# TensorE's instruction order fixed to the order of tracing beside five MLP blocks of a two-layer transformer kernel

## The chip, the cores and the metric

The kernel runs on one core of one Trainium2 chip, as one program in one launch. The metric is the device time of that launch in microseconds, the median of several runs. The profiled execution is one more run; its own time stands beside its span below.

The engines are called by the profile's names: PE is TensorE (matmuls), PEld its weight loads, DVE is VectorE, ACT ScalarE, POOL GpSimd, SP the engine that issues all loads and stores here. Each works through a list of its own, in order; where one needs a result of another it waits on a semaphore.

## The reference

Two layers over 2,048 tokens (32 sequences of 64) of width 512, everything in float32. Cut to what matters:

```
# layer 0: rms norm scaled by a condition, 8 query heads of 64 on one key head, rope, then a gated MLP
h = ada_rms(x, cond, ln1_w, ln1_tw)
q, k, v = h @ Wq.T, h @ Wk.T, h @ Wv.T
x = x + softmax(rope(q) @ rope(k).T / 8) @ v @ Wo.T
h = ada_rms(x, cond, ln2_w, ln2_tw)
x = x + (silu(h @ Wg.T) * (h @ Wu.T)) @ Wd.T          # inner width 2048
# layer 1: layer norm with scale and shift from the condition, 16 heads of 32 on 4 latent key heads
h = (x - mean(x)) * rsqrt(var(x) + eps) * (1 + scale) + shift
c = h @ Wkd.T;  k, v = c @ Wku.T, c @ Wvu.T;  q = h @ Wq.T
out = x + softmax(masked(rope(q) @ rope(k).T / sqrt(32))) @ v @ Wo.T
```

Each sequence attends to itself alone, so scores and contexts are many small products.

## The kernel before, in words

**Tiling.** The tokens are cut into eight units of 256 (four sequences each), kept transposed: features on the partitions, tokens along the row. A unit goes through `attention0` (layer 0), then the MLP, then `attention1` (layer 1). The MLP works on blocks, `BLOCKS = ((0,), (1, 2), (3, 4), (5, 6), (7,))`: three blocks of two units and a block of one at either end.

**The MLP.** Each weight product is done by seven products of half size instead of eight (the names `P1` to `P7`), with sums of weight quarters and of inputs prepared by DVE and POOL. `gate_up_first` issues the four EARLIER products of a group and the partial sums that follow (line 1068 on ACT, lines 1069, 1070 and 1089 on DVE). `gate_up_last` issues the three LATER ones, which add onto the same PSUM regions and so have to wait until those sums have been read; then come line 1098 and 1107 on DVE, `silu` (1101, 1102) on ACT and `gated` (1109 to 1112) on POOL. `down` does the same for the third weight, with `gu` and `down` as names of the PSUM tiles. All of these matmuls are issued by line 1053, in `multiply`. In block 0 DVE also makes the sums of the weights (lines 331 to 334) and the rotation angles of later units (line 421).

**Narrow matmuls.** Scores (`sc`: line 792 in layer 0, 982 in layer 1) and contexts (`cx`: 813 and 1012) contract over 64 rows only. They are traced so that neighbours differ in the half of the rows they use: the score loops go over `for r, sc in enumerate(banks)` innermost, with `of = slice(r * HD0, (r + 1) * HD0)`, and so do the contexts. Between scores and contexts lies the softmax: lines 654, 655, 662, 663 on DVE, 660 on ACT, the scaling 664 on POOL (tile `p`), then the transposes `pp` on PE (669) and the copy `pT` on ACT (670). The output product is `po` (line 634), the context copies `cT` are 823 and 1024.

**What sets the order.** Three things. First the tracing: `Order.run` takes pieces from generators (`mlp(j)`, `attention0` of the units of the next block, and the `chain` of `attention1` of units that are finished), each with a cost and a latency written by hand, and so interleaves their instructions. Second the framework's scheduler: it makes from what was traced the list of each engine, and may put an instruction ahead of others that were traced before it when it takes those to be not ready yet. Third the helper `ordered(tc, engine)`: it ties every instruction of that engine, traced inside it, to the one traced before, with a dependence that needs no semaphore, so that the scheduler has to keep their order:

```
    for one, other in zip(mine, mine[1:]):
        tc.add_manual_dep(other, one.name, info, reason="order")
```

Before the change it is used on PE in two places, around the hand-written orders `FIRST` (the head) and `LAST` (the tail), and on SP for the first loads. The five calls of `order.run` beside the MLP blocks (line 1305) are not inside it: there the scheduler moves PE's instructions. The lists of the other engines are the scheduler's in either kernel, and so are SP's, whose weight loads wait for the matmuls that free their slots.

Of the kernel before, what the change touches and what calls it, by code (L numbers as in the profile page):

```python
# [103 lines left out]
@contextmanager  # L104
def ordered(tc, engine):

    traced = tc.nc.cur_bb.bb.instructions
    start = len(traced)
    yield
    mine = [i for i in traced[start:] if i.engine == engine]  # L110
    info = mybir.DependencyInfo(mybir.DependencyClass.NoSync, mybir.DependencyReason.DATA)
    for one, other in zip(mine, mine[1:]):
        tc.add_manual_dep(other, one.name, info, reason="order")
# [18 lines left out]
def two_blocks(ctx: ExitStack, tc: tile.TileContext, a: dict, out: bass.AP):  # L132
# [328 lines left out]
    def turning():  # L461
        for i, units in enumerate(TURNED):
            yield from angles(units, 4.0 if i else 1.5)
            if i + 1 < len(TURNED):
                load_positions(TURNED[i + 1])
# [702 lines left out]
    def mlp(j):  # L1168
        cost = 1.8 if len(BLOCKS[j]) == 1 else 3.5
        for g in GROUPS:  # L1170
            gate = gate_up_first(j, 0, g[0])
            yield cost, 0.0
            up = gate_up_first(j, 1, g[0])
            yield cost, 0.0
            for q in g:
                gate_up_last(j, 0, q, *gate)
                silu(gate[0], gate[2])
                yield 0.75 * cost, 0.0
                more = None
                if q != g[-1]:  # L1180
                    more = gate_up_first(j, 0, q + 1)
                    yield cost, 0.0
                gate_up_last(j, 1, q, *up)
                gated(j, q, up[0], up[2], gate[2])
                yield 0.75 * cost, 0.0
                gate = more
                if q != g[-1]:
                    up = gate_up_first(j, 1, q + 1)
                    yield cost, 0.0
            yield from down(j, g)  # L1190
# [3 lines left out]
    order = Order()  # L1194
# [47 lines left out]
    rest = [ahead, Job(turning(), 1.0)]  # L1242
# [31 lines left out]
    def some(pieces, n):  # L1274

        for cost, latency in pieces:
            n -= cost > 0
            yield cost, latency
            if not n:
                return  # L1280

    def in_turn(units):
        for u in units:
            while u not in x_units or u not in turned_units:
                yield 0.0, 1.0
            yield from attention0(u, {"ring": "0"})

    chain = Job(behind(), 0.8 * A1)
    for j, units in enumerate(BLOCKS):
        now = Job(mlp(j), M * len(units))  # L1290
        jobs = [now, *rest]
        must = [now]
        if j == 0:
            must.append(ahead)
        if j + 1 < len(BLOCKS):
            more = [u for u in BLOCKS[j + 1] if u > 1]
            must.append(Job(in_turn(more), A0 * len(more)))
            jobs.append(must[-1])
        if j == 1:
            jobs.append(chain)  # L1300
        if j == len(BLOCKS) - 1:
            jobs.append(Job(some(sixth, EARLY), 5.0))
        chain.total = 0.8 * A1 * (len(BLOCKS[j - 1]) if j else 1)
        chain.done = 0.0
        rest = order.run(jobs, until=tuple(must))
    order.run(rest)
    homes["now"] = everywhere
    room7 = {
# [100 lines left out]
```

## Time and profile before

| what | value |
|---|---|
| median of 3 runs | 1018.92 us (1017.89 to 1021.43) |
| the profiled run's own time | 1017.48 us |
| its span, from the first to the last instruction | 1015.7 us |
| PE busy | 985.1 us (97%), 6,710 records |
| DVE / POOL / ACT busy | 543.5 / 426.0 / 300.5 us |
| PE idle, all waits | some 30 us |
| mean granted clock of PE | 0.995 |

Stretches of 25 us show where PE is not full (the rest of the span between 200 and 825 us has it at 24.2 or more of 25):

| stretch, us | PE busy | DVE busy | granted clock |
|---|---|---|---|
| 0 to 50 (head) | 44.8 of 50 | 37.6 | 1.00 |
| 75 to 100 (block 0) | 21.1 of 25 | 23.4 | 1.00 |
| 125 to 150 (block 0) | 20.4 | 24.6 | 0.94 |
| 150 to 175 (block 0) | 22.0 | 18.0 | 0.92 |
| 825 to 850 (end of block 3) | 21.9 | 3.9 | 0.93 |
| 1000 to 1016 (tail) | 11.6 of 16 | 3.7 | 1.00 |

How to read it: times are from one execution. A float32 matmul leaves two records, a transpose one, so "x32" of scores are 16 matmuls. The ends of matmul records are modelled and overlap the next start; durations of stretches are therefore taken here from start to start. A 128x256 product takes 0.432 us from its start to the next one's (two records of 0.216), a 128x128 one 0.223 us.

### The profile page before, as it was taken

What the parts mean: (1) busy time and instruction counts of PE and PEld (TensorE: products, weight loads), DVE (VectorE), ACT (ScalarE), POOL (GpSimd) and SP (SyncE); (2) the same over time, 40 slices, a digit from 0 to 9 for tenths busy, and PEclk for the clock granted to TensorE, in tenths of its full rate; (3) what the DMA queues carried; (4) which work ended last, traced back from release to release, by engine and by line L of the source; (5) the groups of instructions that cost most, each with busy time, mean ns of one, the idle gap of its engine ahead of it and who ended that gap; (6) DMA issues with size and microseconds to landing.
All of it is one profiled execution on the core that took longest, in us unless ns stands there. A gap on an engine that the chain in (4) does not pass through costs nothing.

```text
span 1015.7 us, 17477 instructions
## 1 busy us (share of the span) xinstructions
PE 985.1 (97%) x6710; PEld 853.2 (84%) x6710; DVE 543.5 (54%) x1188; ACT 300.5 (30%) x550; POOL 426.0 (42%) x439
## 2 busy tenths in 40 slices
PE   8998988999999999999999999999999989999998
PEld 7788878988888888888888887888788869998986
DVE  5779997665364342654455361564335533654274
ACT  4434133123223211234313341322413321425032
POOL 5336265444523333534344333554234523843251
PEclk9999999999999999999999999999999999999999
DMA  7936375623222345222232234323233324746201
GB/s 272 325 126 218 128 230 173 211 88 132 72 69 83 130 138 171 86 94 85 94 115 94 73 124 129 120 89 120 80 95 107 130 88 158 248 157 222 90 2 42
DMA packets 82642, 132.23 MB, mean 130 GB/s; under 512 B 8832, under 2 KB 48512, under 8 KB 82176
## 3 DMA queue, kind: packets, MB, share of 16 engines
q1 hardware_dynamic: 82560, 131.12, 38.9%
q8 instruction: 53, 0.87, 0.3%
q14 instruction: 29, 0.24, 0.1%
HBM read 114.31 MB, written 16.78 MB: 129 GB/s over the span
## 4 chain that ended last, share of the span: by engine, by line
PE 83%; DVE 9%; DMA 2%; POOL 2%; issue 2%; ACT 2%; SPq 0%; POOLq 0%; DVEq 0%; ACTq 0%
PE gu L1053 34%; PE down L1053 17%; PE po L634 10%; PE q L634 10%; PE sc L982 2%; DVE stays L421 2%; PE pp L669 2%; PE lat L634 1%; DMA stays<-in_wmlp 1%; PE cx L1012 1%; PE kv L634 1%; ACT cT L823 1%; PE cx L813 1%; PE sc L792 1%; PE tab L502 1%
## 5 line engine op out<-in xcount | busy, mean ns | idle before, releaser
L1053 PE MATMUL gu<-h,stays 128*128 128x256 f32 (+1 forms) x1280 | 259.9, 341 | 10.5 <-issue 5.6
L1053 PEld LDWEIGHTS gu<-h,stays 128*128 128x128 f32 x1280 | 207.7, 191 | 36.3 <-issue 12.0
L1053 PE MATMUL down<-stays 128*128 128x256 f32 (+1 forms) x1120 | 210.2, 341 | 0.0
L1053 PEld LDWEIGHTS down<-stays 128*128 128x128 f32 x1120 | 177.2, 191 | 24.2 <-issue 5.4
L1053 PE MATMUL gu<-hc,stays 128*128 128x256 f32 (+1 forms) x960 | 195.5, 339 | 0.4 <-DVE hc L860 0.2
L1053 PEld LDWEIGHTS gu<-hc,stays 128*128 128x128 f32 x960 | 157.5, 191 | 17.4 <-DVE hc L860 0.6
L634 PE MATMUL po<-cT,stays 128*128 128x256 f32 x480 | 109.5, 385 | 2.8 <-ACT cT L823 2.6
L634 PE MATMUL q<-h,stays 128*128 128x256 f32 x480 | 109.2, 380 | 0.0
L634 PEld LDWEIGHTS po<-cT,stays 128*128 128x128 f32 x480 | 91.5, 193 | 16.9 <-ACT cT L823 3.9
L1109 POOL TENSOR_TENSOR stays<-gate,stays 128x768 f32<-128x768 f32 (+1 forms) x40 | 53.1, 1329 | 113.6 <-DVE stays L1098 106.8
L634 PEld LDWEIGHTS q<-h,stays 128*128 128x128 f32 x480 | 90.2, 190 | 11.9
L1068 ACT COPY e<-gu 128x256 f32<-128x256 f32 (+1 forms) x80 | 26.1, 328 | 188.7 <-PE gu L1053 188.6
L664 POOL TENSOR_TENSOR p<-p,sm 128x512 f32<-128x512 f32 x40 | 41.7, 1059 | 89.5 <-DVE sm L663 88.1
L645 POOL TENSOR_TENSOR qT<-u_q,v_q 128x512 f32<-128x512 f32 x30 | 38.1, 1271 | 87.6 <-DVE v_q L644 87.6
L690 DVE TENSOR_TENSOR x<-x,po 128x512 f32<-128x512 f32 x28 | 19.2, 687 | 102.3 <-PE po L634 102.3
L1069 DVE TENSOR_TENSOR u<-e,gu 128x256 f32<-128x256 f32 (+1 forms) x80 | 28.8, 360 | 62.6 <-ACT e L1068 62.6
L621 POOL TENSOR_TENSOR h<-x,stays 128x1024 f32<-128x1024 f32 x12 | 23.0, 1914 | 66.9 <-DVE x L690 48.8
L1110 POOL TENSOR_TENSOR stays<-stays 128x512 f32<-128x512 f32 (+1 forms) x40 | 45.0, 1126 | 4.1 <-DVE stays L1107 1.4
L1070 DVE TENSOR_TENSOR w<-u,gu 128x256 f32<-128x256 f32 (+1 forms) x80 | 29.1, 364 | 31.0 <-PE gu L1053 30.3
L576 DVE RECIPROCAL stays<-stays 128x256 f32<-128x256 f32 (+1 forms) x23 | 35.4, 1540 | 14.6 <-ACT stays L575 14.5
L654 DVE TENSOR_REDUCE mx<-sc 128x8 f32<-128x512 f32 (+1 forms) x52 | 31.4, 642 | 20.9 <-PE sc L982 16.9
L1098 DVE TENSOR_TENSOR gate<-gu,u 128x512 f32<-128x512 f32 (+1 forms) x40 | 23.2, 580 | 32.8 <-PE gu L1053 32.4
(223 smaller groups left out, 1268.6 us busy)
## 6 DMA issues: line engine op xcount, KB each, us to landing
stays<-sums SPq DMA_DIRECT2D x96, 384.0 KB, 3.0
stays<-in_wmlp SPq DMA_DIRECT2D x120, 256.0 KB, 3.0
stays<-in_wmlp SPq DMA_DIRECT2D x120, 128.0 KB, 2.5
stays<-sums SPq DMA_DIRECT2D x96, 128.0 KB, 2.3
sums<-stays SPq DMA_DIRECT2D x24, 384.0 KB, 3.0
mod<-in_mod SPq DMA_DIRECT2D x8, 512.0 KB, 5.2
x<-in_x SPq DMA_DIRECT2D x8, 512.0 KB, 5.8
a<-in_wmlp SPq DMA_DIRECT2D x24, 128.0 KB, 3.4
```

Of the source, the lines that this page charges most:

```text
L576: nc.vector.reciprocal(r, r)
L634: nc.tensor.matmul(ps, w[:, k, cols], h[:, k, :], start=(k == 0), stop=(k == KC - 1))
L645: nc.gpsimd.tensor_tensor(dst, u, v, ALU.add)
L654: nc.vector.tensor_reduce(mx, s3, AX.X, ALU.max)
L664: nc.gpsimd.tensor_tensor(p8, p8, sm.unsqueeze(2).to_broadcast(wide), ALU.mult)
L1053: nc.tensor.matmul(ps[REGION[p]][:, c], w[:, slot, cols], moving, start=opening and ps.opens(p, c, k), stop=p in LATER, skip_group_check=True,
L1068: nc.scalar.copy(e, ps[0])
L1069: nc.vector.tensor_tensor(u2, e, ps[1], ALU.add)
L1070: nc.vector.tensor_tensor(w2, u2, ps[2], ALU.add)
L1098: nc.vector.tensor_tensor(c12_21, ps.late_pair()[:, :, 0], u2.to_broadcast([P, 2, ht]), ALU.add)
L1109: e.tensor_tensor(act[:, 2:5], gate[:, 1:4], act[:, 2:5], ALU.mult)
L1110: e.tensor_tensor(act[:, 0:4:2], act[:, 2:4], act[:, 1:3], ALU.subtract)
```

## The change

Around the one call of `order.run` inside the loop over the blocks stands now `ordered(tc, mybir.EngineType.PE)`:

```diff
         chain.total = 0.8 * A1 * (len(BLOCKS[j - 1]) if j else 1)
         chain.done = 0.0
-        rest = order.run(jobs, until=tuple(must))
+        with ordered(tc, mybir.EngineType.PE):
+            rest = order.run(jobs, until=tuple(must))
     order.run(rest)
```

No instruction is added or taken away, and none changes its shape. In each of the five passes PE's instructions, traced by that call, stand in its list as they were traced; that covers the MLP block and the attention work interleaved with it. From one pass to the next nothing is tied, so the first matmuls of a block can still move into the end of the block before. The scheduler makes the other lists anew around this one.

## The prediction

> All times are microseconds (us) of the profiled execution: 1017.48 in all, 1015.7 of span. Its own time lies 1.44 under the median of the runs, 1018.92; what I work out from its rows as a difference is added to that median. About 3.06 (0.3%) is what a measurement of this kernel can tell from no change.
>
> **What bounds the kernel now.** I read the page's busy line first, then its chain of work that ended last, then stretches of 25 us, then the rows of PE at the places where the two programs' lists for PE differ.
>
> ```profile
> PE 985.1 (97%) x6710; PEld 853.2 (84%) x6710; DVE 543.5 (54%) x1188; ACT 300.5 (30%) x550; POOL 426.0 (42%) x439
> ...
> PE 83%; DVE 9%; DMA 2%; POOL 2%; issue 2%; ACT 2%; SPq 0%; POOLq 0%; DVEq 0%; ACTq 0%
> ```
>
> PE sets the end: 97% busy, 83% of the chain. The next lines have, for each stretch, its length, then busy time (and records) of PE, weight loads, DVE, ACT and POOL, then PE's granted clock, DMA share and GB/s.
>
> ```profile
> 125.00:150.00 25.00, 20.35 (x153) 17.87 (x152) 24.60 (x61) 9.93 (x21) 15.55 (x18) 0.94 0.79 253
> 350.00:375.00 25.00, 25.00 (x117) 21.99 (x117) 11.56 (x20) 3.57 (x7) 8.86 (x8) 1.00 0.41 137
> ```
>
> In block 0 DVE is the one without a gap (24.60 of 25) and PE waits for it; in the middle blocks PE is full and the others have half their time free. So there a change of PE's order is worth what it does to the products' own time, plus any new idle time; some 30 us of idle in all, at few places, is what the order can lose or win.
>
> **Part 1, what the order restores.** Products on the whole array cost the same in any order, 0.432 (128x256) or 0.223 (128x128) from start to start; moving them gains nothing. The narrow ones do not. PE's rows have start, duration, engine, line, tile and record count (two to a matmul):
>
> ```profile
> 460.05 1.10 PE L982 MATMUL sc<-kb,qT 64*64 64x128 f32 x32
> 461.08 0.70 PE L1053 MATMUL gu<-h,stays 128*128 128x256 f32 x2
> ...
> 580.68 1.09 PE L982 MATMUL sc<-kb,qT 64*64 64x128 f32 x16
> 581.70 1.56 PE L1053 MATMUL gu<-h,stays 128*128 128x256 f32 x6
> 583.20 1.09 PE L982 MATMUL sc<-kb,qT 64*64 64x128 f32 x16
> 584.22 0.70 PE L1053 MATMUL gu<-h,stays 128*128 128x256 f32 x2
> ```
>
> Sixteen score products traced in alternation take 461.08 - 460.05 = 1.03. Where the scheduler has let one PSUM tile's eight go first and the other's later, each half is in one half of the rows throughout and takes as long alone: 584.22 - 580.68 = 3.54, less three foreign products (3 x 0.432 = 1.30) and less 1.03: 1.21 lost. The same subtraction (intact twin of the same tile: scores of layer 1 1.03, of layer 0 1.09; contexts 1.03 and 0.59) at the eleven split groups of blocks 1 to 3: .51 (296.36), .26 (309.41), .74 (335.88), .74 (481.53), .48 (483.29), .74 (492.78), 1.19 (558.84), 1.21 (580.68), .74 (612.13), .39 (718.14), .74 (726.74): 7.74. Held to the trace, all eleven alternate again: **-7.7**. Changes between narrow and whole products cost 0.1 to 0.24 each in these rows, and some four to eight fewer remain: **-0.8** (0 to -1.5). The split group at 116 lies in block 0 and is counted with it.
>
> **Part 2, what the order makes PE wait for.** I walked PE's new list with the times at which the trace shows each input done.
>
> Block 0, 59 to 165: PE meets two more waits (+1.0 at 104 to 121, +1.7 at 127 to 133, where it stands 5.5 for line 1089 of the fifth group while before it filled this with other products). DVE's list keeps its work and DVE its lack of gaps, and PE anyway waits 3.01 at 164.94 for DVE; a PE that is 2.6 later finds that wait shorter by as much. Cover lost, the price is +2.6; if DVE gets its inputs in a better order, a gain of like size: **0** (-2.5 to +2.6). SP's list changes most here, with the parking of weight sums (lines 342, 344) moved among loads; DMA share is 0.79 in this stretch and the loads stay as many, so it stands in the same bounds. In the later blocks a few loads swap neighbours.
>
> 174 to 200: the products of `hc` now come before others, so PE waits 1.9 for line 860 (177.43) where before it filled all but 0.6; and line 571 of ACT moves behind other functions, one more table load of 1.28, off PE's path: **+1.2**.
>
> Small waits for the copies `pT` and `cT` of ACT, earlier covered by MLP products: .38, .35, .47, .56, .28 at 258, 298, 472, 490, 563: **+2.0**.
>
> Place A, 606 to 612: the list takes the first products of block 3 earlier, whose weights landed at 608.81: PE arrives at 606.86, waits 1.95. POOL's list now has lines 1109 to 1112 (1.55 + 1.27 + .73 + .73, from first start to last end 4.55 at the twin place 822.50) ahead of both 664 that PE's `pp` need; scores are traced 1.5 earlier in PE's list, so POOL is done at some 610.2 and 611.2: waits of .96 and .15. Sum 3.06 against .20 + .63 before: **+2.2** (0 to +4).
>
> Unit 7's softmax, 719 to 737: `pp` waits for 664 of 725.77 and `po` for the copy of line 823, no other products between: **+1.9** (0 to 2.4, the copy's length).
>
> Place B, 815 to 834: `pp` waits 2.78 + .34 now; walked, 3.7: **+0.5**.
>
> Place C, 882, is the largest:
>
> ```profile
> 882.14 1.95 PE L1053 MATMUL down<-stays 128*128 128x128 f32 x16
> 884.75 1.99 PE L634 MATMUL lat<-h,stays 128*128 128x256 f32 x8 [0.67 <-POOL h L900]
> ...
> 887.45 1.05 PE L1053 MATMUL gu<-h,stays 128*128 128x128 f32 x8
> ```
>
> ```profile
> 882.22 1.75 DVE L576 RECIPROCAL stays<-stays 128x256 f32<-128x256 f32 x1
> 883.88 0.23 DVE L1069 TENSOR_TENSOR u<-e,gu 128x128 f32<-128x128 f32 x1
> 884.43 1.36 DVE L897 TENSOR_TENSOR h<-h,stays 128x1024 f32<-128x1024 f32 x1 [0.31 <-DVE u L1069]
> 885.71 0.28 DVE L1070 TENSOR_TENSOR w<-u,gu 128x128 f32<-128x128 f32 x1
> 886.10 0.28 DVE L1089 TENSOR_TENSOR gate<-w,gu 128x128 f32<-128x128 f32 x1
> ```
>
> The three LATER products need line 1089, done at 886.38, because a reciprocal of 1.75 and a line 897 of 1.36 of the attention stand between DVE's steps, and DVE's list is the same there in both programs. Before, eight `down`, four `lat` and two `q` ran in the meantime; now they stand behind the LATER products. PE arrives at 882.14 and stands until 886.38: 4.24 for .67: **+3.6** (0 if the reciprocal falls elsewhere, 4.2 if the later .67 stays).
>
> **The clock.** These stretches lie on the throttle's grid of 3.41:
>
> ```profile
> 92.62:96.03 3.41, 1.60 (x13) 1.42 (x12) 3.38 (x11) 2.11 (x2) 2.84 (x5) 1.00 0.74 257
> 96.03:99.45 3.42, 2.88 (x26) 2.88 (x26) 2.70 (x6) 3.37 (x6) 2.68 (x3) 1.00 0.45 158
> 143.82:147.23 3.41, 1.51 (x9) 1.20 (x8) 3.26 (x7) 2.32 (x5) 1.57 (x2) 1.00 0.90 312
> 147.23:150.65 3.42, 3.42 (x10) 2.71 (x9) 3.14 (x10) 0.51 (x2) 3.10 (x5) 0.50 0.72 268
> ```
>
> After one with PE busy for 1.51 of 3.41 the next is granted 0.50; after 1.60 it is not. Half speed for a full window costs 1.6 (this happens three times before: 147.23, 167.71, 829.90). Place C leaves 1.0 busy in one window: +1.5. Place A leaves about 1.6, on the edge: half of 1.6. **+2.3** (0 to 4.8).
>
> [...]
>
> **Sum.** -7.7 - 0.8 + 0 + 1.2 + 2.0 + 2.2 + 1.9 + 0.5 + 3.6 + 2.3 = +5.2: span 1020.9, profiled run 1022.7, median 1018.92 + 5.2 = **1024.1**; this case's own range is 1020 to 1029.
>
> **Rivals.** *The waits at A and C do not arise* (chance 0.25): DVE and POOL follow the new PE, which is up to 8 ahead by then, so the gate of line 1089 comes before the reciprocal, and POOL's four before `p`. For it: DVE and POOL have half their time free there. Against it: the reciprocal's place in DVE's list is unchanged, and POOL's list has the four first. Without A (2.2), C (3.6) and their clock (2.3): 5.2 - 8.1 = -2.9: 1016.0, not slower. *Block 0 decides* (0.15): the waits there are not absorbed at 165 because DVE's own steps for the next group wait for the late products; from the point where PE's delay exceeds 3.01 it moves everything after it: +2.6, and two more half-speed windows at 1.6: +5.8 more, 1029.9. For it: DVE at 24.60 of 25 can make nothing good. *The change does little* (0.05), because the scheduler already keeps nearly the traced order: 1018.9. Against: 725 lines of difference in PE's list.
>
> **Chances.** The forecast has 0.55, a tenth of it under 1021.98. Faster (under 1015.86) is half of the first rival, 0.12; the same is its other half, the last rival and that tenth, 0.23; slower 0.65. The range 1015 to 1032 leaves out a third of the first rival and of the second, and little else.
>
> **What would show it.** Right: score and context groups all at 1.03, 1.09 or 0.59; PE idle before line 1053 near 882 by some 4, released by line 1089, with a clock of 0.5 after; PE's busy time down by 6 to 9 outside half-speed windows, idle up by 10 or more. Wrong: PE idle in blocks 1 to 4 unchanged; split groups still there; stretches in block 0 that end more than 2 later at `hc` of block 1; a wait on a weight load that lands later than now.

## The result, and the profile after

The changed kernel takes 1031.97 us (median of 6 runs, 1030.53 to 1034.45); the kernel before took 1018.4 beside it. The ratio is 1.0135 with a 95% interval of 1.011 to 1.0161: slower by some 13.6 us, where 5.2 had been forecast. The profiled run has a span of 1029.6 against 1015.7.

The busy line of the changed kernel's page:

```profile
PE 982.6 (95%) x6710; PEld 857.6 (83%) x6710; DVE 550.9 (54%) x1188; ACT 299.8 (29%) x550; POOL 426.6 (41%) x439
```

PE is busy for 2.5 less than before (985.1) in a span that is 13.9 longer. The two figures hide a third, the clock. These are the stretches in which the changed kernel's PE was granted half speed, except the line with a clock of 1.00, which is the window ahead of the last of them. The six begin at whole multiples of 3.413 from each other (119.45 to 894.28); a window is one such step. The columns are length, busy time (records) of PE, weight loads, DVE, ACT and POOL, then the granted clock, DMA share and GB/s:

```profile
119.45:122.86 3.41, 3.41 (x17) 3.41 (x17) 1.44 (x4) 0.00 (x0) 0.54 (x1) 0.50 0.20 46
...
133.10:139.93 6.83, 4.39 (x20) 4.42 (x21) 5.57 (x17) 0.69 (x2) 2.64 (x3) 0.50 0.47 176
...
170.65:177.48 6.83, 5.90 (x28) 5.93 (x28) 4.46 (x8) 0.69 (x2) 2.53 (x4) 0.50 0.35 126
...
614.38:617.79 3.41, 3.41 (x12) 2.70 (x11) 0.00 (x0) 1.17 (x2) 0.32 (x1) 0.50 0.16 38
...
836.25:839.66 3.41, 3.29 (x11) 2.80 (x11) 0.00 (x0) 1.05 (x2) 0.09 (x1) 0.50 0.00 0
890.87:894.28 3.41, 0.59 (x6) 0.39 (x4) 3.41 (x5) 0.27 (x1) 3.41 (x3) 1.00 0.85 250
894.28:901.11 6.83, 5.48 (x26) 5.51 (x27) 2.16 (x7) 1.97 (x3) 4.02 (x4) 0.50 0.22 67
```

PE works for 25.9 in the six half-speed stretches (3.41 + 4.39 + 5.90 + 3.41 + 3.29 + 5.48), which are nine windows. Before there were three windows, with 10.0 of work: the one at 147.23, shown above, and these two:

```profile
167.71:171.13 3.42, 3.18 (x15) 3.21 (x16) 1.05 (x4) 0.69 (x2) 0.73 (x1) 0.50 0.44 169
...
829.90:833.31 3.41, 3.41 (x22) 1.86 (x21) 0.00 (x0) 1.13 (x3) 0.00 (x0) 0.50 0.00 0
```

By the granted clock of 0.50, half of PE's working time there is counted as lost. That is an estimate; for the last stretch it gives 2.7, and an experiment below measures 2.4. With it the span, up to PE's last record, divides without rest (the differences are taken before rounding):

| part | before | after | difference |
|---|---|---|---|
| PE's busy time, had all of it been at full speed | 985.1 - 5.0 = 980.1 | 982.6 - 12.9 = 969.7 | -10.5 |
| what half speed added | 5.0 | 12.9 | +7.9 |
| PE idle, up to its last record | 27.5 | 44.0 | +16.5 |
| sum | 1012.6 | 1026.6 | +13.9 |

The change did make PE's work cheaper, by 10.5. It paid more than twice that in waits and in clock.

Where it was paid is read from the points at which both lists of PE have issued the same instructions so far; there the starts can be subtracted. The offset is by how much the changed kernel is behind at such a point:

| from - to (time before) | forecast | shown | offset at its end |
|---|---|---|---|
| start - 194, block 0 | +1.2 | +4.7 | +4.7 |
| 194 - 207, start of block 1 | 0 | +1.1 | +5.9 |
| 207 - 602, blocks 1 and 2 | -3.9 | -3.6 | +2.3 |
| 602 - 639, place A | +2.3 | +3.9 | +6.2 |
| 639 - 743, to the end of unit 7's softmax | +0.8 | +2.8 | +9.0 |
| 743 - 858, place B | +0.5 | +0.2 | +9.2 |
| 858 - 890, place C | +5.1 | +6.1 | +15.2 |
| 890 - end | 0 | -1.3 | +13.9 |

(The forecast's column is its terms by place, the clock's among them and the split groups where they lie: the +1.2 for `hc`, whose wait it put at 177, in the first row, -5.9 and +2.0 of small waits in the third, -0.7 + 2.2 + 0.8 in the fourth. Its -0.8 for fewer switches has no place.)

The same division, done at these points, shows what the large rows consist of. Block 0 is +3.4 of idle time, +3.6 of half speed and -2.2 of work. Place A is +3.0, +1.7 and -0.8. Place C is +3.5, +2.7 and -0.2.

The narrow groups alternate again, as forecast. A score group of the changed kernel, whose twin had been split before, from PE's rows (start, duration, line, records):

```profile
584.50 1.10 PE L982 MATMUL sc<-kb,qT 64*64 64x128 f32 x32
585.53 1.99 PE L1053 MATMUL gu<-h,stays 128*128 128x256 f32 x8
```

It takes 585.53 - 584.50 = 1.03 and has nothing between its products.

### The profile page after: what moved, and what is told of

Read it like the earlier page. It is cut to its first block, busy times and chain, and to the rows that moved or that the text cites. A ratio compares the mean times of both kernels' runs of the same rounds, so it can differ in the third digit from the quotient of the medians.

```text
span 1029.6 us, 17482 instructions
## 1 busy us (share of the span) xinstructions
PE 982.6 (95%) x6710; PEld 857.6 (83%) x6710; DVE 550.9 (54%) x1188; ACT 299.8 (29%) x550; POOL 426.6 (41%) x439
## 4 chain that ended last, share of the span: by engine, by line
PE 82%; DVE 10%; issue 2%; ACT 2%; DMA 2%; POOL 1%; SPq 0%; POOLq 0%; DVEq 0%; ACTq 0%
PE gu L1053 35%; PE down L1053 17%; PE po L634 10%; PE q L634 9%; DVE stays L421 2%; PE pp L669 1%; PE lat L634 1%; PE sc L982 1%; DMA stays<-in_wmlp 1%; PE kv L634 1%; ACT cT L823 1%; DVE sm L662 1%; PE cx L1012 1%; POOL p L664 1%; DVE mx L654 1%
## 5 line engine op out<-in xcount | busy, mean ns | idle before, releaser
L1053 PEld LDWEIGHTS gu<-h,stays 128*128 128x128 f32 x1280 | 211.0, 195 | 44.1 <-issue 19.7
L1053 PEld LDWEIGHTS down<-stays 128*128 128x128 f32 x1120 | 182.1, 196 | 23.9 <-issue 2.8
L1156 POOL TENSOR_TENSOR x<-x,c 128x256 f32<-128x256 f32 x16 | 11.6, 726 | 82.1 <-DVE c L1143 82.1
```

Of the source, the lines that this page charges most:

```text
L1053: nc.tensor.matmul(ps[REGION[p]][:, c], w[:, slot, cols], moving, start=opening and ps.opens(p, c, k), stop=p in LATER, skip_group_check=True,
```

## The experiments

"Against before" in the expectations is the difference to the kernel before; each ratio is to runs of it on the same chip. Where a kernel is compared with the changed one, it is by these differences: the changed kernel has +13.6.

### The tie in some blocks only

```diff
-        with ordered(tc, mybir.EngineType.PE):
+        with ordered(tc, mybir.EngineType.PE) if j == 0 else nullcontext():
             rest = order.run(jobs, until=tuple(must))
```

and the same with `0 < j < 4` and with `j == 4`. Block 0 alone:

> PE's list is held to the order of tracing in block 0 alone; the other four passes are left to the scheduler. Theory (the loss lies at a few places, each a wait of PE and the half-speed window or windows behind it): the loss of block 0 as the two profiles show it at common points of the lists, +4.7 at 194, so 4.7 slower than before (3 to 7), with PE's gap of 4.6 near 131 and half speed after it. Rival A (block 0 is absorbed, as the prediction took it; the offset seen there is given back later): within 1.5 of before. Rival B (the loss comes from tying all passes, and one alone does little): within 1.5 as well, but then the runs with blocks 1 to 3 and with block 4 alone are also within 1.5.

Measured: 1022.47, ratio 1.0051 (1.0032 to 1.0071), against 1017.55: +4.9. PE waits 4.81 near 138 and half speed follows for 6.83. The theory held; the prediction's own term for block 0 falls, and so does rival B.

Blocks 1 to 3 alone:

> PE's list is held in blocks 1, 2 and 3 alone. Theory: between the points 206.6 and 857.7 of before the offset grows from 5.9 to 9.2, so +3.3 (1 to 6): restored narrow groups are worth some -8 to -10 and the waits for POOL's p at the ends of blocks 2 and 3 and in unit 7's softmax, with their half-speed windows, +11 to +13. Rival (the gain of narrow groups was overrated and the waits are small): within 1.5 of before, and PE's busy time not lower.

Measured: 1025.51, ratio 1.0082 (1.0057 to 1.0108): +8.0, more than either said (the theory had +1 to +6; the interval begins at +5.8). The work at full speed is 972.0, 8.2 less than before, so the gain is there. The idle time is 12.8 more. One wait of it does not show in the changed kernel: 1.98 for `hc` (line 860) near 176, with a half-speed window behind it. There PE came to this place late because of block 0's waits, and stood for 0.27 only. The blocks' losses are not additive: 4.9 + 8.0 + 5.1 make 18, and the change costs 13.6. This wait, which hides behind an earlier one, and its window are one reason; whether they are all of the 4.4 is not shown.

Block 4 alone:

> PE's list is held in block 4 alone. Theory: the wait of 4.2 for line 1089 and two half-speed windows behind it come back, and the tail gives 1.1 back: +5 (4 to 6.5). Rival (the wait near 890 of the changed kernel comes only because blocks before it shifted DVE's and POOL's work against PE's): within 1.5 of before.

Measured: 1022.61, ratio 1.005 (1.0028 to 1.0071): +5.1. The wait is 4.18 and 6.83 of half speed follow, as in the changed kernel. It needs no help from the blocks before it.

### The narrow loops alone

Each loop gets a chain of its own, with nothing else tied:

```diff
-            for n in range(KC * len(ts)):
+            for n in held(tc, range(KC * len(ts))):
...
+def held(tc, steps):
+    with ordered(tc, mybir.EngineType.PE):
+        yield from steps
```

and so the other three loops.

> Nothing of the change; instead each loop of scores and of contexts is held by itself to its order of tracing, so that neighbours alternate between the halves of the rows, while all other products stay free for the scheduler. Theory (PE's busy time at full speed is some 10 lower in the changed kernel because narrow groups alternate again, and the loss is all waits and clock): 6 to 10 faster than before. Rival A (what is saved comes back as waits, since the scheduler had split the groups at places where something was late): within 2 of before. Rival B (the subtraction was wrong and halves don't matter): within 1, with PE's busy time unchanged.

Measured: 1019.49, ratio 1.0018 (0.9997 to 1.0039). No gain: the theory's number missed. The time is where rival A put it, but not for its reason, as the idle time is only 2.2 over before's. PE's work at full speed is 979.9, as before (980.1), which was the sign of rival B. Summed over the records, from each start to the next and half speed counted half, the four narrow lines take 51.9 before, 44.7 in the changed kernel, and 50.6 here, while line 1053 takes 1.9 more than before. PE's rows of this kernel show why:

```profile
584.55 0.43 PE L982 MATMUL sc<-kb,qT 64*64 64x128 f32 x2
584.91 1.99 PE L1053 MATMUL gu<-h,stays 128*128 128x256 f32 x8
586.84 1.10 PE L982 MATMUL sc<-kb,qT 64*64 64x128 f32 x30
```

The order within the group is kept, but the scheduler still puts whole products into it. Counted over the span, the narrow products stand in 57 pieces (of one line, with nothing between) before, in 48 in the changed kernel and in 61 here. Order alone did bring something among the scores of line 982, which take 19.0 before, 17.7 here and 16.9 in the changed kernel: two groups that stood whole before, but in another order, fall from 1.51 (at 483.29) and 1.25 (at 600.76) to 1.03. The contexts of line 1012 gained nothing (13.2, 13.4 and 10.4). There pieces with different contents took nearly the same: a single product set apart 0.54 (486.07 here), four products of one half 0.57 (482.72 before), the whole group of eight 0.59. So rival B is right about these contexts, and wrong about the scores. The order of the narrow ones alone did not suffice here: 50.6 in 61 pieces, against 44.7 in 48 under the tie of the whole list.

### What PE stands at, taken out of the chain

The names of the products that stay free are collected at the place that issues them (`free(tc, n)` takes the last n of PE), and `ordered` leaves them out:

```diff
-    mine = [i for i in traced[start:] if i.engine == engine]
+    mine = [i for i in traced[start:] if i.engine == engine and i.name not in FREE]
...
-        done_with("l", what)
+        done_with("l", what); len(BLOCKS[j]) == 1 and free(tc, 6)
```

> The change, but the LATER products of the MLP in blocks 0 and 4 (units alone) are left out of the chain of ties; all other products of the five passes stay tied. Theory (in these blocks the tie makes PE stand in front of LATER products until DVE's line 1089, and half-speed windows follow): the wait of 4.2 near 891 falls under 1, with its two half-speed windows (2.7 by the busy time in them, halved); in block 0 the wait of 4.6 near 131 shrinks. 6 to 10 less than the changed kernel, so +4 to +8 against before. Rival (block 0's and block 4's loss comes from the lists of DVE, POOL and SP that the scheduler made anew, not from PE standing at these products): within 2 of the changed kernel, +12 to +15.

Measured: 1024.14, ratio 1.0071 (1.0042 to 1.01): +6.7, 6.9 less than the changed kernel. The scheduler puts `down`, `lat` and two products of `q` ahead of block 4's LATER products again, and the wait there is .67. The wait of 4.6 in block 0 becomes 0.66 and 1.15. The theory held in the whole time, and at place C, where PE's offset no longer grows (10.85 ahead of it and behind). In block 0 it held for the wait alone: up to the point at 194 the idle time is 4.0 over before's, where the changed kernel has 3.4, because the wait for `hc` of 1.98 comes up again behind. The wait of 3.01, which before the change ends at 167.95, stays too and ends at 170.50.

### POOL's order alone

```diff
-        e.tensor_tensor(act[:, 2:5], gate[:, 1:4], act[:, 2:5], ALU.mult)
+        with after(tc, mybir.EngineType.Pool, P_LAST[0]) if q == 7 and j in (2, 3) else nullcontext(): e.tensor_tensor(act[:, 2:5], gate[:, 1:4], act[:, 2:5], ALU.mult)
```

`P_LAST[0]` is the last line 664 that was traced.

> The change, with one thing altered on POOL alone: at the ends of blocks 2 and 3 line 664 of the last softmax stands ahead of lines 1109 to 1112 of the eighth group; the lists of PE, DVE, ACT and SP stay those of the changed kernel. Theory (the order that the scheduler gave POOL around the held PE makes PE's transposes wait 2.7 and 3.4, and half speed follows, 1.7 each): 6 to 9 less than the changed kernel, +5 to +8 against before; what is left are waits under 1 for DVE's sums. Rival (down's second half needs lines 1109 to 1112, which are now 2 later, and PE waits there instead): within 2 of the changed kernel.

Measured: 1022.98, ratio 1.0064 (1.004 to 1.0088): +5.6, 8.0 less than the changed kernel. Place A in the rows of POOL, first of the changed kernel, then of this one:

```profile
607.24 1.86 POOL L1109 TENSOR_TENSOR stays<-gate,stays 128x768 f32<-128x768 f32 x1 [7.35 <-DVE stays L1098]
...
612.66 2.04 POOL L664 TENSOR_TENSOR p<-p,sm 128x512 f32<-128x512 f32 x2
```

```profile
609.91 2.04 POOL L664 TENSOR_TENSOR p<-p,sm 128x512 f32<-128x512 f32 x2 [9.86 <-DVE sm L663]
611.90 1.54 POOL L1109 TENSOR_TENSOR stays<-gate,stays 128x768 f32<-128x768 f32 x1
```

and PE at that place, again the changed kernel and then this one:

```profile
613.76 0.66 PE L669 MATMUL pp<-stays,p 128*128 128x128 f32 x4 [2.69 <-POOL p L664]
```

```profile
611.05 0.61 PE L669 MATMUL pp<-stays,p 128*128 128x128 f32 x4
```

The wait of 2.69 is gone, that of 3.42 at place B is 0.53, and no half speed follows either (the mean granted clock is 0.990 in place of 0.985). PE's list is the same in both, so these two waits are not the price of a held list as such: the scheduler gave POOL four operations of `gated` first. At place B it had done so before the change too, with a wait of 2.78; why it did so now at place A no run shows.

### Both together

> Both of the alterations of the first and third run of this call together on the change. Theory (the places are independent): the two savings add, 12 to 19 less than the changed kernel, so between 1 and -5 against before, with the narrow groups still intact (their 7 kept). Rival (block 0 stays behind, since DVE sets its pace whatever PE's list is): +3 to +6.

Measured: 1015.78, ratio 0.998 (0.9956 to 1.0004): -1.6, 15.2 less than the changed kernel. The savings add (6.9 + 8.0). PE's work at full speed is 971.2, so the gain is kept; half speed falls on 6.8 of its work, less than before the change (10.0), in one profile of each. What remains is idle time, 34.6 against 27.5.

### The clock by itself

`fill(n)` issues n products of a constant with itself, ahead of LATER products at which PE waits:

```diff
-                gate_up_last(j, 0, q, *gate)
+                fill(FILL.get((j, 0, q), 0)); gate_up_last(j, 0, q, *gate)
...
+FILL = {(0, 0, 4): 18, (0, 1, 7): 13, (4, 0, 3): 16}
```

> The change, with products of a constant with itself (128x128, their result read by nobody) put ahead of the three groups of LATER products at which PE stands longest in blocks 0 and 4: 18, 13 and 16 of them for waits of 4.6, 3.2 and 4.2. They make no wait shorter. Theory (the waits cost twice, once as idle time and once as half speed after it): the half-speed windows behind the three waits are not granted, 2.2 + 2.9 + 2.7 by the busy time in them, halved: 5 to 8 less than the changed kernel, +6 to +9 against before. Rival (half speed is no consequence of the waits, or what follows waits for other engines anyway): within 1.5 of the changed kernel, or slower.

Measured: 1035.27, ratio 1.0183 (1.0155 to 1.0211): +17.9, slower still. At the three places no half speed follows any more (the LATER products last 1.13 each time, and 2.05, 2.05 and 2.04 in the changed kernel); but the scheduler made DVE's and SP's lists anew, and two waits appear that were not there: PE stands 2.82 for DVE's line 332 (until 180.09) and 2.88 for its line 884 (until 202.81). As a test of the whole time this failed. The next kernel has the fill at place C alone, where only the sixteen products are added and no other list changes:

> The changed kernel with sixteen products of a constant with itself (read by nobody) ahead of the LATER products in block 4 where PE stands 4.2 (near 891), and nothing else altered on any engine. Theory (the wait costs a second time by the half speed that follows it): the wait stays, in fill and rest, and the stretch from the first LATER product to the first product of lat takes 4.8 in place of 7.1, so the time is 2 to 3 less than the changed kernel, +10.5 to +12 against before. Rival (half speed is not caused by the idle wait): the stretch stays at 7.1 and the time within 1 of the changed kernel.

PE's rows of the changed kernel, and then of this one:

```profile
895.63 2.04 PE L1053 MATMUL gu<-h,stays 128*128 128x128 f32 x8 [4.17 <-issue]
...
902.77 1.46 PE L634 MATMUL lat<-h,stays 128*128 128x256 f32 x6
```

```profile
890.91 3.74 PE L205 MATMUL fill<-stays 128*128 128x128 f32 x32
895.25 1.13 PE L1053 MATMUL gu<-h,stays 128*128 128x128 f32 x8 [0.60 <-issue]
...
900.01 1.89 PE L634 MATMUL lat<-h,stays 128*128 128x256 f32 x8
```

The LATER products start equally late after the fill as after the wait (4.79 and 4.78 behind the start of the last EARLIER ones), and the windows lie alike: counted on in steps of 3.41 from the half speed at place B (836.25, and 835.88 with the fill), one begins 4.76 ahead of the LATER products in either kernel. It has PE busy for 0.59 without the fill and throughout with it. The stretch to `lat`, with the same products in it, takes 4.76 (900.01 - 895.25) in place of 7.14 (902.77 - 895.63). The 2.4 is half speed alone, and with the wait filled it is gone. The two profiled runs differ by as much (spans of 1026.8 and 1029.6). In the whole time it is not resolved: 1030.28, ratio 1.0131 (1.0108 to 1.0153) beside 1.0135, which is +13.0 beside +13.6, so by the median alone the rival's number came.

### A version that beats both

To the kernel with both alterations two more were added:

```diff
-        done_with("f", what)
+        done_with("f", what); j and not m and not q and free(tc, 8)
...
-            yield 0.5 * len(ts), 5.0 * ts[0] if lean else 10.0
+            yield 0.5 * len(ts), 5.0 * ts[0] if lean else 10.0 if u < 7 else 14.0
```

> The kernel with POOL's order at the ends of blocks 2 and 3 and with the LATER products of blocks 0 and 4 free, and two more waits taken out: the first four products of each block after block 0 are free as well (PE waited 1.98 for hc near 177 and 1.18 for a weight load near 608), and unit 7's softmax of layer 0 has a latency of 14 in place of 10 in the tracing, so that its transposes are traced behind four more products of down (PE waited 2.6 near 725). Theory (what is left of the loss is waits at named places, and the narrow groups keep their 7): 3 to 5 less than that kernel's 1015.8, so 1011 to 1013, 4 to 7 faster than before. Rival (waits move to the next late thing): within 1.5 of 1015.8.

Measured: 1008.35 against 1017.32, ratio 0.9921 (0.99 to 0.9943), 9.0 faster than before the change and 22.6 less than the changed kernel. The page's busy line:

```profile
PE 973.6 (97%) x6710; PEld 848.8 (84%) x6710; DVE 547.5 (54%) x1188; ACT 299.7 (30%) x550; POOL 425.2 (42%) x439
```

PE's work at full speed is 970.2, its idle time 29.6. The waits of 1.98 and 2.6 are gone; that of 1.17 for the weight load stays. The gain is more than the 4 to 7 that had been expected; at the end of the interval, 0.9943, it is 5.8.

> As the first kernel of this call, but PE is held in blocks 1, 2 and 3 alone; blocks 0 and 4 are left to the scheduler as before the change. Theory (in blocks 0 and 4 the tie brings nothing but waits, the narrow groups that it restores lie in blocks 1 to 3): equal to the first kernel of this call or up to 3 less, the extra wait for DVE's line 1143 near 119 being gone. Rival (block 0 gains too by its restored groups): 1 to 2 more than the first.

Measured: 1012.44, ratio 0.995 (0.993 to 0.997): not equal, but 4.1 more than the first kernel. The theory missed and its rival was nearer: 972.0 of work at full speed against 970.2, and 1.3 more idle. Line 792, to which block 0's split score group belongs, takes 9.3 in place of 8.8. By the profiles this kernel is 1.7 behind the first at 858, ahead of block 4, and 2.8 at the end. So the tie is worth having in the blocks of one unit too, once LATER products are free there; the share of each block is read from one profile.

## Why the prediction was wrong, by its steps

By kind, the forecast of +5.2 was -8.5 of work, +11.4 of idle time and +2.3 of clock; the profile has -10.5, +16.5 and +7.9. The direction was right. The miss is 5.1 of idle time and 5.6 of clock, less 2.0 of work.

**Part 1, what the order restores: right in kind and near in size.** -7.7 for eleven groups and -0.8 for switches were forecast. The narrow lines take 7.2 less (51.9 to 44.7), which includes block 0's group, and the work at full speed 10.5 less, most of the rest in line 1053 (3.3). The run with the loops alone adds that order alone earned 1.3 of the 7.2 (51.9 to 50.6).

**Block 0 at "0 (-2.5 to +2.6)": the first step that failed.** Its argument was that "a PE that is 2.6 later finds that wait shorter by as much". PE did come later, with 3.1 more idle time by 163, but the wait that was to absorb this is 3.23 in place of 3.01. PE's rows, before and then two of the changed kernel:

```profile
167.95 2.05 PE L1053 MATMUL gu<-h,stays 128*128 128x128 f32 x8 [3.01 <-issue]
```

```profile
135.54 2.05 PE L1053 MATMUL gu<-h,stays 128*128 128x128 f32 x8 [4.63 <-issue]
...
171.58 2.05 PE L1053 MATMUL gu<-h,stays 128*128 128x128 f32 x8 [3.23 <-issue]
```

("issue" means that the profile names no releaser; line 1089 of DVE ends 0.1 ahead of each.) The argument took DVE's times as fixed, but that wait's input starts at PE itself. ACT's copy of the group, then the end of the chain on DVE, before:

```profile
162.90 0.27 ACT L1068 COPY e<-gu 128x128 f32<-128x128 f32 x1 [1.90 <-PE gu L1053]
```

```profile
167.57 0.28 DVE L1089 TENSOR_TENSOR stays<-w,gu 128x128 f32<-128x128 f32 x1
```

and in the changed kernel:

```profile
166.55 0.27 ACT L1068 COPY e<-gu 128x128 f32<-128x128 f32 x1 [1.91 <-PE gu L1053]
```

```profile
171.21 0.27 DVE L1089 TENSOR_TENSOR stays<-w,gu 128x128 f32<-128x128 f32 x1
```

From ACT's copy, which waits for PE's EARLIER products, to line 1089 it is 4.67 and 4.66. DVE works without a gap in between, but it had itself stood 1.39 for an earlier copy of this kind in both kernels (until 156.94 and 160.59). So the loop has moved with PE as a whole. "DVE its lack of gaps" held from 125 to 150 only: behind that, before the change, DVE stands 2.71 for PE's `po` (154.86) and 2.37 for its `gu` (170.89).

In the changed kernel DVE has a gap earlier as well, which the prediction had bounded with the loads. It stands 3.12 for a weight load, where it stood 0.55; before, and then in the changed kernel:

```profile
122.46 0.43 DVE L331 TENSOR_TENSOR stays<-a,stays 128x256 f32<-128x256 f32 x1 [0.55 <-DMA stays<-in_wmlp]
```

```profile
124.11 0.42 DVE L331 TENSOR_TENSOR stays<-a,stays 128x256 f32<-128x256 f32 x1 [3.12 <-DMA stays<-in_wmlp]
```

Line 1089 of the fifth group then starts at 135.16 in place of 132.61. How much of PE's wait of 4.63 is due to this load and how much to the held list no run separates; with LATER products free DVE stands 3.05 for it and PE no longer 4.63.

The second rival, "Block 0 decides", named the mechanism, with DVE's own steps waiting for the late products. It priced block 0 at 5.8, with two more half-speed windows in it; block 0 alone costs 4.9. Its time, 1029.9, is nearer to the measured 1031.97 than the forecast's 1024.1.

**The clock at +2.3: the second step, a term mis-sized.** It was +7.9. The prediction counted one window for place C and half a one for A: 1.5 and 0.8, where 2.7 and 1.7 are shown. Three waits that lay across the edge of a window (4.63, 3.23 and 4.17) each had two windows at half speed, and block 0's three stretches were not counted at all, against two single windows there before: +3.6. The kernel with the fill at place C shows that the cost there belongs to the wait (the stretch behind it takes 4.76 in place of 7.14). At place A the waits are 1.18 and 2.69, PE is busy for 0.72 of 3.41 in the window ahead, and half speed follows at 614.38.

**`hc` at +1.2: the number came by luck.** The start of block 1 does cost +1.1, but PE stands only 0.27 for line 860, and between 175 and 200 no idle time is added. The +1.1 lies behind 200 and is chiefly a wait of 0.82 for DVE's line 756, which the prediction did not have. The wait for line 860 shows in the kernels where PE comes to it earlier (1.98). ACT has no table load more in sum, 66 in either kernel (and its line there is 575; 571 is PE's).

**Place C: right** in its wait (4.17 shown, 4.24 forecast) and its release by line 1089 (which ends at 895.52; PE starts at 895.63), short by the second window. **Unit 7's softmax: too small**, waits of 2.61 and 0.58 for 1.9 (at most 2.4). **Place A: too small in idle time**, 1.18 + 2.69 for 3.06; POOL's four took 1.86, 1.59, 1.06 and .72, not the 1.55, 1.27, .73 and .73 of their rows before. **Place B: +0.5 forecast, +0.2 shown.** A wait of 0.99 near 660, which no step of the prediction has, is most of the 1.2 lost between 639 and 655.

The first rival, that the waits at A and C do not arise, fell: they arose in full.

## What to carry to other kernels

A scheduler's freedom did two things at once here: it filled waits (0.67 at place C, 4.17 without it) and it tore apart groups that cost less when whole (51.9 on the narrow lines, 44.7 without it). Before taking it away, list which products stand behind a result that the same engine started, and leave those free. A wait whose input goes back to the waiting engine need not shrink when that engine is late (3.01 became 3.23 here), so do not count on it to absorb an earlier delay. Price a wait of PE twice, by its length and by the half-speed windows behind it (4.17 and 2.4 at place C).

## What was not expected of the hardware

The clock differed between runs at the same work. The head is the same program in the kernel before and in the one with block 0 tied, with the same wait of 1.58 ahead of these products; in the rows of PE, before and then in the other:

```profile
12.01 2.14 PE L634 MATMUL kv<-h,stays 128*128 128x256 f32 x8 [1.58 <-POOL h L617]
14.08 0.65 PE L583 MATMUL ms_a<-sq_a,stays 128*32 128x64 f32 x32
```

```profile
12.03 3.05 PE L634 MATMUL kv<-h,stays 128*128 128x256 f32 x8 [1.58 <-POOL h L617]
15.00 1.08 PE L583 MATMUL ms_a<-sq_a,stays 128*32 128x64 f32 x32
```

In the first the granted clock is 1.00 there and the four products take 2.07 up to the next start; in the second they take 2.97. One profile therefore shows one run: those of the kernel before spread from 1012.63, with a mean granted clock of 1.000, to 1023.76, with 0.988. What exactly makes a window fall to half speed stays open: one with 1.80 of 3.41 busy (116.04 in the changed kernel) was followed by it, one with 1.60 (92.62 before) was not.

At place A two operations took longer in the changed kernel than in the one with POOL's order altered. Line 860 on DVE took 2.03 while POOL ran lines 1109 and 1110, and 0.68 in the other, where POOL was idle then. POOL's line 1109 took 1.86 and 1.54.
